# Tokenizer and attention of a vision tower: instruction order written by hand in place of the framework's scheduler

## The chip, the cores and the metric

The kernel runs on one core of one Trainium2 chip. A core has a matrix engine (TensorE, "PE" in the profile; its weight loads are listed apart as "PEld"), a vector engine (VectorE, "DVE"), a scalar engine (ScalarE, "ACT"), a general engine (GpSimd, "POOL") and a queue engine for transfers (SyncE, "SP"). Each engine runs its own stream of instructions in order and waits on semaphores for the others. On-chip memory is SBUF; PE writes into PSUM, eight banks of 128 partitions by 512 floats. The metric is the device time of one launch in microseconds (us), the median of several runs. Smaller is better.

## What is computed

32 images of 256 x 256 pixels become 256 tokens of 256 features each, and two transformer layers follow, all in float32. The change touches only the tokenizer, the attention of layer 0, and the first moments of layer 0's feed-forward part. Cut to these, the reference is:

```
# tokenizer: 16 x 16 patches of 3 channels -> 768 numbers per token
h = einsum('bnk,ek->bne', patches, W) + b

# layer 0, gated attention on layernorm(h); H = 512, S = 128
norm  = norm(x) * rsqrt(d);  xn = x / max(norm, 1e-5) * g
uv    = silu(xn @ W_uv + b_uv)                 # 256 -> 512 + 512 + 128
u, v, base = uv[:512], uv[512:1024], uv[1024:]
q, k  = base * gamma[0] + beta[0], base * gamma[1] + beta[1]
attn  = square(relu(q @ k.T * rsqrt(S)))
h     = h + (u * (attn @ v)) @ W_o + b_o

# layer 0, feed-forward with a router, on x = layernorm(h)
weights = x @ wr + br
sel     = the 127 tokens of each image with the largest weights
h       = h + x + (mlp(x[sel]) * weights[sel] at sel, 0 elsewhere)
# layer 1: a phase memory (part D) and a mixture of attention heads (part E)
...
```

## The kernel before

The parts follow one another: A is the tokenizer, B is layer 0's attention, C its feed-forward part, D and E are layer 1. The activations `H[b]` of all 32 images stay in SBUF for the whole run. The kernel is written in a framework that finds the waits by itself. It can also choose the order of the instructions within each engine's stream, from its own estimate of times. Where the code opens a `manual_schedule` for an engine, that engine's instructions keep the order in which they are written.

In the kernel before, part A is in written order for PE, ACT and SP only (DVE and POOL are ordered by the framework). Part B is ordered wholly by the framework. Parts C, D and E are in written order on all engines.

Part A handles one image at a time: 12 products (6 blocks of the 768 inputs, 2 halves of the tokens), an eviction with bias, and the statistics of the norm. Part B works on pairs of images. `unit_b` is a generator; each `yield` ends one step of a pair, and the steps of successive pairs are handed out so that up to five pairs are under way. The transposes and the products all go through `bank()`, a ring of the 8 PSUM banks.

```
def transposed(xT, xs, copy):              # 8 transposes into 2 banks, 2 copies
    for k in range(2):
        p = bank()
        for j, x in enumerate(xs):
            for c in range(NC):
                nc.tensor.transpose(p[:, ...], x[:, c, k * P : (k + 1) * P], ident)
        copy(k, xT[:, k, :], p[:, 0:w])    # copy_split: k = 0 on ACT, k = 1 on DVE

def unit_b(b0):                            # images b0 and b0 + 1
    xs = []
    for j in range(2):
        x = p4.tile([P, NC, D], F32, name="bx")
        normed(x, b0 + j, st_b)            # 2 tensor_scalar on DVE
        xs.append(x)
        nc.gpsimd.tensor_tensor(H[b0 + j], H[b0 + j], <b_o>, ALU.add)
    transposed(xT, xs, copy_split)
    <base: 2 products 128 x 512, silu on ACT>     # needs both halves of xT
    <q and k: 2 tensor_scalar on DVE>
    yield
    <scores: 4 products 128 x 256, relu on ACT, square on POOL>
    <gates uT: 8 products 128 x 512, silu on ACT>
    <values vs: 8 products 128 x 512, bias on DVE, silu on ACT>
    yield
    <gated: 16 products 128 x 256, times uT on DVE -> gT>
    if b0 == B - 2:
        turn_c(0, quads[0], 0)             # part C: transposes of the first four images
    <output: 16 products 128 x 256, added to H on DVE; statistics; power on POOL>
    yield
    normed_c[b0] = [norm_c(b0 + j) for j in range(2)]
    yield
    ranks(b0)                              # bank pw; rank_c for both images
    if b0 in (2, 6): first_ranks(b0 - 2, quads[b0 // 4], 0)

def norm_c(b):                             # layernorm for the router, and its weights w
    x = px.tile([P, NC, D], F32, name="cx", bufs=6)
    normed(x, b, st_c)
    nc.gpsimd.tensor_tensor(H[b], H[b], x, ALU.add)
    <per half: scalar_tensor_tensor with the row wr, summed into w, through a scratch ctmp>
    return x, w

def rank_c(b, x, w, pw):
    for c in range(NC):                    # w across the columns: 2 transposes on PE
        nc.tensor.transpose(pw[:, c * P : (c + 1) * P], w[:, c : c + 1].to_broadcast([P, P]), ident)
    <per half: 2 scalar_tensor_tensor on DVE that read pw, into ctmp, and a rank>
    <3 small DVE instructions; 2 indirect DMAs on POOL that store x by rank>
```

At the start of part C, in written order:

```
for t in range(END_C):
    if t < 2:
        ranks(B - 4 + 2 * t)               # pairs 28 and 30, which part B left
    if t == 0:
        normed_c[B - 2] = [norm_c(B - 2 + j) for j in range(2)]
    step_c(t)                              # t = 0: hidden_c(.., 0), t = 1: hidden_c(.., 1), ...
```

`hidden_c` is 8 products of 128 x 512 for each half, with a GELU on ACT. In the profile, line L115 is the helper of all products, L188 the transposes of `transposed`, L193 and L195 its copies on ACT and DVE, L174 the norms, L350 the transposes of `w`, L355 and L357 the ranks on DVE.

Of the kernel before, what the change touches and what calls it, by code (L numbers as in the profile page):

```python
# [33 lines left out]
F32 = mybir.dt.float32  # L34
# [6 lines left out]
P = 128  # L41
# [38 lines left out]
def vit_tower(tc, a, out):  # L80
# [115 lines left out]

    def one_step(active):
        return [g for g in active if next(g, g) is not g]

    def phase(unit, images, steps):  # L200

        active = []
        for b in range(0, B, images):
            active = one_step([unit(b)] + active)
        for _ in range(steps - 1):
            active = one_step(active)
        return active  # L210


    region, passing_x = ExitStack(), ExitStack()
# [33 lines left out]

    patches = a["patches"].rearrange("(k p) t -> p k t", p=P)
    with (
        tc.tile_pool(name="a_w", bufs=1) as pw,  # L250
        tc.tile_pool(name="a_x", bufs=6) as pp,
        tc.manual_schedule(engines={ENG.PE, ENG.Activation, ENG.SP}),
    ):
# [33 lines left out]

        loaded = []
        st_b = new_stats("b")

        def unit_a(b):
            if b == 0:
                ps = [bank() for _ in range(NC)]
                for k in range(n_k):
                    for c in range(NC):
                        mm(ps[c][:, 0:D], x0[k][:, c * P : (c + 1) * P], tokW[k], k == 0, k == n_k - 1)
                for c in range(NC):
                    nc.vector.tensor_tensor(H[b][:, c, :], ps[c][:, 0:D], row_a("tok_b"), ALU.add)
            else:
                x, p = xs_a.pop(b), bank()  # L300
                for c in range(NC):
                    for k in range(n_k):
                        mm(p[:, c * D : (c + 1) * D], x[:, k, c * P : (c + 1) * P], tokW[k], k == 0, k == n_k - 1)
                nc.vector.tensor_tensor(
                    H[b], p.rearrange("p (c d) -> p c d", c=NC), over(row_a("tok_b"), [P, NC, D], 1), ALU.add
                )
                if b + 5 < B:
                    load_patches(b + 5)
            st, _, i = at(st_b, b)
            for c in range(NC):  # L310
                stats(st, i, c, H[b][:, c, :])
            if b == 4:
                loaded.extend(layer_0_weights())
            if b % 2:
                factors_b(b - 1)
            yield

        def factors_b(b):


            st, rs, i = at(st_b, b)
            q = slice(i * NC, (i + 2) * NC)
# [4 lines left out]
            nc.gpsimd.tensor_tensor(rs[:, q], rs[:, q], minus_half[:, 0 : 2 * NC], ALU.pow)  # L327
            nc.vector.scalar_tensor_tensor(rs[:, q], low, 1e5, rs[:, q], ALU.mult, ALU.min)
            nc.vector.tensor_scalar(rs[:, q], rs[:, q], col("attn_g"), None, ALU.mult)

        phase(unit_a, 1, 2)
        wuv, row_b, wo, row_c, before, w1 = loaded

    def norm_c(b):
        x = px.tile([P, NC, D], F32, name="cx", bufs=6)
        normed(x, b, st_c)
        nc.gpsimd.tensor_tensor(H[b], H[b], x, ALU.add)

# [7 lines left out]
        return x, w  # L346

    def rank_c(b, x, w, pw):
        for c in range(NC):
            nc.tensor.transpose(pw[:, c * P : (c + 1) * P], w[:, c : c + 1].to_broadcast([P, P]), ident)  # L350

# [18 lines left out]
    with (  # L370
# [3 lines left out]
        st_c = new_stats("c")  # L374
        scale = 1.0 / math.sqrt(128.0)

        def unit_b(b0):
            xs = []
            for j in range(2):
                x = p4.tile([P, NC, D], F32, name="bx")  # L380
                normed(x, b0 + j, st_b)
                xs.append(x)
                nc.gpsimd.tensor_tensor(
                    H[b0 + j], H[b0 + j], over(row_b("b_o"), [P, NC, D], 1), ALU.add
                )
            xT = p2.tile([P, 2, 2 * N], F32, name="bxT")
            transposed(xT, xs, copy_split)

            base = p2.tile([P, 2 * N], F32, name="base")
            p = bank()  # L390
            for k in range(2):
                mm(p, wuv[:, k, 1024:1152], xT[:, k, :], k == 0, k == 1)
            nc.scalar.activation(base, p, AF.Silu, bias=col("b_base"))
            q = p2.tile([P, 2 * N], F32, name="bq")
            nc.vector.tensor_scalar(q, base, col("gamma", 0), col("beta", 0), ALU.mult, ALU.add)
            kk = p2.tile([P, 2 * N], F32, name="bk")
            nc.vector.tensor_scalar(kk, base, col("gamma", 1), col("beta", 1), ALU.mult, ALU.add)

            yield
            attn = []  # L400
            for j in range(2):
                p = bank()
                for m in range(NC):
                    mm(p[:, m * N : (m + 1) * N], kk[:, j * N + m * P : j * N + (m + 1) * P], q[:, j * N : (j + 1) * N])
                r = p2.tile([P, NC, N], F32, name="relu")
                nc.scalar.activation(r.rearrange("p m n -> p (m n)"), p, AF.Relu, scale=scale)
                t = p4.tile([P, NC, N], F32, name="attn")
                nc.gpsimd.tensor_tensor(t, r, r, ALU.mult)
                attn.append(t)

            uT = p2.tile([P, 4, 2 * N], F32, name="uT")
            for hc in range(4):
                p = bank()
                for k in range(2):
                    mm(p, wuv[:, k, hc * P : (hc + 1) * P], xT[:, k, :], k == 0, k == 1)
                nc.scalar.activation(uT[:, hc, :], p, AF.Silu, bias=col("b_u", hc))
            vs = []
            for tb in range(2 * NC):
                p = bank()
                for k in range(2):  # L420
                    mm(p, xT[:, k, tb * P : (tb + 1) * P], wuv[:, k, 512:1024], k == 0, k == 1)
                v = p4.tile([P, 512], F32, name="bv", bufs=8)
                nc.vector.tensor_tensor(v, p, row_b("b_v"), ALU.add)
                nc.scalar.activation(v, v, AF.Silu)
                vs.append(v)

            yield
            gTs = []
            for j in range(2):
                gT = p2.tile([P, 4, N], F32, name="gT")  # L430
                for half in range(2):
                    p = bank()
                    for h in range(2):
                        hc = 2 * half + h
                        for m in range(NC):
                            mm(
                                p[:, h * N : (h + 1) * N], vs[j * NC + m][:, hc * P : (hc + 1) * P],
                                attn[j][:, m, :], m == 0, m == NC - 1,
                            )
                    nc.vector.tensor_tensor(  # L440
                        gT[:, 2 * half : 2 * half + 2, :], p.rearrange("p (h n) -> p h n", h=2),
                        uT[:, 2 * half : 2 * half + 2, j * N : (j + 1) * N], ALU.mult,
                    )
                gTs.append(gT)
            if b0 == B - 2:
                turn_c(0, quads[0], 0)
            for j in range(2):
                b, gT = b0 + j, gTs[j]
                p = bank()
# [5 lines left out]
                for c in range(NC):  # L455
                    stats(st, i, c, H[b][:, c, :])

            pow_rstd_of(st_c, b0, 2)

            yield  # L460
            normed_c[b0] = [norm_c(b0 + j) for j in range(2)]

            yield
            ranks(b0)
            if b0 in (2, 6):
                first_ranks(b0 - 2, quads[b0 // 4], 0)

        normed_c = {}

        def ranks(b0):  # L470
            pw = bank()
            for j in range(2):
                rank_c(b0 + j, *normed_c[b0][j], pw[:, j * N : (j + 1) * N])


        phase(unit_b, 2, 3)
    region_b.close()

# [248 lines left out]
    with region_c:  # L727
# [20 lines left out]
        def fetch(b0, s, half):  # L748
            s.y = s.y if half else []
            for b in range(b0 + 2 * half, b0 + 2 * half + 2):  # L750
                y = px.tile([P, NC, D], F32, name="cx", bufs=6)
                for c in range(NC):
# [31 lines left out]
        preparing = prepare()  # L784
        with tc.manual_schedule(engines={ENG.PE, ENG.DVE, ENG.Activation, ENG.Pool, ENG.SP}):
            for t in range(END_C):
                if t < 2:
                    ranks(B - 4 + 2 * t)
                if t == 0:
                    normed_c[B - 2] = [norm_c(B - 2 + j) for j in range(2)]  # L790
                if t == END_C - 2:
                    norm_d(0, pairs[0], px, "cx", 6)
                step_c(t)
                if t >= 8:
                    next(preparing, None)
        passing.close()
# [5 lines left out]
    with (  # L802
        tc.manual_schedule(engines={ENG.PE, ENG.DVE, ENG.Activation, ENG.Pool, ENG.SP}),
        tc.tile_pool(name="d_2", bufs=2, reuse_waits="tile") as p2,
# [119 lines left out]
    right_d.close()  # L924
    passing_x.close()


# [719 lines left out]
```

## Time and profile before

| | before |
|---|---|
| time, median of 3 runs | 2030.3 us (2027.38 to 2031.56) |
| span of the profiled run | 2025.9 us |
| PE busy | 1953.6 us (96%) |
| DVE / ACT / POOL busy | 1316.5 / 823.9 / 726.8 us |
| PE records | 15108 products and as many weight loads |

A float32 product appears as two records in the trace (the tokenizer's 384 products as 768). [...] the records of a dense stream overlap, so the time that a stream takes is read from its length and not from the sum of durations. In the stage table each row gives, for one stretch, its length, then for PE, PEld, DVE, ACT and POOL the busy us with the number of instructions that started there, then the granted clock of PE (1.00 is full speed), the share of DMA and the GB/s. In the timeline each row gives the start, the length of a merged run of like instructions, engine, line, operation, output<-input and count; in square brackets stand the idle us ahead of it and what ended them.

### The profile page before, as it was taken

What the parts mean: (1) busy time and instruction counts of PE and PEld (TensorE: products, weight loads), DVE (VectorE), ACT (ScalarE), POOL (GpSimd) and SP (SyncE); (2) the same over time, 40 slices, a digit from 0 to 9 for tenths busy, and PEclk for the clock granted to TensorE, in tenths of its full rate; (3) what the DMA queues carried; (4) which work ended last, traced back from release to release, by engine and by line L of the source; (5) the groups of instructions that cost most, each with busy time, mean ns of one, the idle gap of its engine ahead of it and who ended that gap; (6) DMA issues with size and microseconds to landing.
All of it is one profiled execution on the core that took longest, in us unless ns stands there. A gap on an engine that the chain in (4) does not pass through costs nothing.

```text
span 2025.9 us, 37649 instructions
## 1 busy us (share of the span) xinstructions
PE 1953.6 (96%) x15108; PEld 1374.2 (68%) x15108; DVE 1316.5 (65%) x3605; ACT 823.9 (41%) x1549; POOL 726.8 (36%) x692
## 2 busy tenths in 40 slices
PE   9998999999999989999899999999999999999984
PEld 8885676766666757666455555577777777777762
DVE  2335557676665653443556465567889999998986
ACT  0001312122222112212444444377777777777761
POOL 1224215243432342434333433203444443434443
PEclk9999999999999999999899999999999999999996
DMA  9440000000000141221000000001212121221211
GB/s 301 150 139 1 0 0 32 16 27 11 22 13 19 36 147 50 78 68 58 11 0 1 1 1 0 0 23 33 54 49 59 49 59 49 54 54 46 62 49 54
DMA packets 69813, 95.09 MB, mean 47 GB/s; under 512 B 8576, under 2 KB 51200, under 8 KB 69248
## 3 DMA queue, kind: packets, MB, share of 16 engines
q1 hardware_dynamic: 62912, 75.04, 13.0%
q0 software_dynamic: 6144, 16.79, 2.7%
q8 instruction: 121, 1.98, 0.4%
q10 hardware_dynamic: 576, 0.79, 0.1%
q14 instruction: 60, 0.49, 0.1%
HBM read 46.45 MB, written 20.97 MB: 33 GB/s over the span
## 4 chain that ended last, share of the span: by engine, by line
PE 94%; DVE 3%; ACT 1%; DMA 1%; POOL 0%; issue 0%; SPq 0%; ACTq 0%; DVEq 0%
PE bank L115 88%; PE bank L688 2%; PE bank L188 1%; PE bank L1192 1%; PE bank L350 0%; DMA both<-hx 0%; ACT bxT L193 0%; PE bank L241 0%; DVE fout L1201 0%; DMA tokW<-in_tokW_dram 0%; DVE bx L174 0%; DVE ctmp L357 0%; DVE fout L1197 0%; DVE two L1123 0%; DVE ctmp L355 0%
## 5 line engine op out<-in xcount | busy, mean ns | idle before, releaser
L1040 ACT ACTIVATE et<-bank 128x512 f32<-128x512 f32 x384 | 202.3, 598 | 58.5 <-DVE bank L1038 57.9
L115 PEld LDWEIGHTS bank<-ev,et 128*64 128x64 f32 x6144 | 198.4, 137 | 33.3 <-ACT et L1040 20.6
L115 PE MATMUL bank<-ev,et 128*64 128x74 f32 (+1 forms) x6144 | 211.3, 227 | 0.0
L1038 DVE TENSOR_TENSOR bank<-bank,w_tri 128x256 f32<-128x256 f32 (+1 forms) x384 | 173.6, 515 | 55.6 <-PE bank L115 53.7
L1118 POOL TENSOR_TENSOR eo<-eo,gate 128x1024 f32<-128x1024 f32 x64 | 121.9, 1925 | 215.7 <-DVE gate L1115 203.1
L115 PE MATMUL bank<-g,sx 64*128 64x512 f32 (+1 forms) x512 | 191.0, 502 | 1.4 <-ACT g L998 1.4
L115 PE MATMUL bank<-g,sw 64*128 64x512 f32 (+1 forms) x512 | 189.6, 502 | 0.0
L115 PE MATMUL bank<-tokW,patch 128*128 128x256 f32 x768 | 168.0, 382 | 0.3 <-DMA tokW<-in_tokW_dram 0.3
L115 PEld LDWEIGHTS bank<-tokW,patch 128*128 128x128 f32 x768 | 146.8, 191 | 21.6 <-DMA tokW<-in_tokW_dram 1.3
L115 PE MATMUL bank<-bxT,w_wuv 128*128 128x512 f32 x320 | 147.9, 601 | 6.6 <-ACT bxT L193 4.0
L193 ACT COPY bxT<-bank 128x512 f32<-128x512 f32 x16 | 9.4, 586 | 341.4 <-PE bank L188 341.4
L1070 POOL TENSOR_TENSOR hv<-hv,minus_half 128x8 f32<-128x8 f32 x64 | 119.6, 1868 | 5.3
L1056 ACT COPY eo<-bank 128x286 f32<-128x286 f32 x256 | 97.3, 421 | 58.5 <-PE bank L115 52.0
L115 PE MATMUL bank<-wvo,dm 128*128 128x512 f32 x256 | 114.0, 598 | 0.0
L115 PE MATMUL bank<-xsel,w_w 128*128 128x512 f32 x256 | 113.4, 601 | 0.0
L115 PE MATMUL bank<-attn,bv 128*128 128x256 f32 x512 | 113.3, 379 | 0.0
L115 PE MATMUL bank<-w_wo,gT 128*128 128x256 f32 x512 | 113.1, 379 | 0.0
L115 PE MATMUL bank<-w_w,hT 128*128 128x256 f32 x512 | 113.1, 379 | 0.0
L115 PE MATMUL bank<-w_wuv,bxT 128*128 128x512 f32 x256 | 112.5, 592 | 0.0
L115 PEld LDWEIGHTS bank<-attn,bv 128*128 128x128 f32 x512 | 97.1, 190 | 19.5 <-issue 6.7
L115 PEld LDWEIGHTS bank<-w_w,hT 128*128 128x128 f32 x512 | 96.7, 190 | 15.8 <-issue 3.4
L1069 POOL TENSOR_SCALAR hv<-ranges 128x8 f32<-128x8 f32 x64 | 39.1, 610 | 189.8 <-DVE ranges L1131 189.6
(258 smaller groups left out, 3861.8 us busy)
## 6 DMA issues: line engine op xcount, KB each, us to landing
patch<-in_patches_dram SPq DMA_DIRECT2D x31, 768.0 KB, 4.8
sw<-sx SPq DMA_DIRECT2D x64, 128.0 KB, 2.4
both<-fxT SPq DMA_DIRECT2D x64, 128.0 KB, 2.4
both<-hx SPq DMA_DIRECT2D x64, 128.0 KB, 2.3
out_dram<-fout SPq DMA_DIRECT2D x32, 256.0 KB, 2.4
cs<-ranked SPq DMA_DIRECT2D x32, 128.0 KB, 3.8
results<-cy SPq DMA_DIRECT2D x32, 128.0 KB, 1.7
w_w<-in_w_dram SPq DMA_DIRECT2D x2, 1024.0 KB, 6.1
```

The source lines that it names most:

```text
L115: nc.tensor.matmul(o, lhsT, rhs, start=first, stop=last)
L188: nc.tensor.transpose(p[:, o : o + P], x[:, c, k * P : (k + 1) * P], ident)
L193: nc.scalar.copy(o, i)
L688: nc.tensor.transpose(p[:, o : o + P], x[:, c, k * P : (k + 1) * P], ident)
L1038: nc.vector.tensor_tensor(own, own, over(tri, [P, n_e, P], 1), ALU.add)
L1040: nc.scalar.activation(t, p, AF.Exp)
L1056: nc.scalar.copy(im.o[:, c * NH + n, 0:OC], p[:, 0:OC])
L1069: nc.gpsimd.tensor_scalar(v, x, 1.0 / HD, 1e-8, ALU.mult, ALU.add)
L1070: nc.gpsimd.tensor_tensor(v, v, minus_half, ALU.pow)
L1118: nc.gpsimd.tensor_tensor(im.mix[k], im.mix[k], over(im.gate[:, :, 2 * k : 2 * k + 2], [P, NC * NH, 2, HD], 3), ALU.mult)
L1192: nc.tensor.transpose(im.po[:, o : o + P], im.fT[:, k, c * P : (c + 1) * P], ident)
```

## The change

All of the kernel from the tokenizer on is put in written order for PE, DVE, ACT, POOL and SP. For that, part B's generator becomes separate functions, one for each piece of a pair's work, and a loop over steps calls them in a chosen order. Four things are meant by that order:

- The norm of a pair (`norm_b`) is written in the middle of the step before the one that transposes it. Pair 0's and pair 1's norms are done inside the tokenizer, and pair 0's transposes, base, queries and keys are written ahead of the tokenizer's last image.
- The router weights of both images of a pair are transposed in one go (`turn_weights`) ahead of the scores, and the ranks that read them come after.
- The scores of the older pair are written between the transposes and the base product of the newer pair.
- The router's norms (`norms_c`) are written ahead of the values' evictions; for pair 28 they come ahead of the last output.

No instruction's arithmetic changes. The tiles of the norm in B move from a pool of four (`bx`) to the shared pool `cx`, which grows from 6 to 8. Pair 0's tiles borrow space of part C (`xsel`, `cs`).

```
+    by_hand.enter_context(tc.manual_schedule(engines={ENG.PE, ENG.DVE, ENG.Activation, ENG.Pool, ENG.SP}))
...
+        for b in range(B):                          # the tokenizer's loop
+            if b == B - 1:
+                half = [p0.tile(..., name="cs", bufs=2) ... for _ in range(2)]
+                turn_b(0, pairs_b[0], p0, "xsel")
+                base_b(0, pairs_b[0], half[0][:, 0 : 2 * N])
+                queries_b(0, pairs_b[0], half[0][:, 2 * N :], half[1][:, 0 : 2 * N])
+            unit_a(b)
+            if b == 4:
+                wuv, row_b, wo, row_c, before, w1 = layer_0_weights()
+            if b % 2:
+                powers = powers_b(b - 1)
+            elif b:
+                factors_b(*powers)
+            if b in (B - 6, B - 4):
+                u = (b - B + 6) // 2
+                norm_b(2 * u, pairs_b[u])
+                bias_b(2 * u, pairs_b[u])
...
-        x = px.tile([P, NC, D], F32, name="cx", bufs=6)
+        x = px.tile([P, NC, D], F32, name="cx", bufs=8)
...
-        phase(unit_b, 2, 3)
+        for t in range(B // 2 + 2):
+            new, old, older, next_one = pair(t) if t else None, pair(t - 1), pair(t - 2), pair(t + 1)
+            next_one = next_one if t else None
+            if new:
+                turn_b(*new, p2, "bxT")
+            if t >= 4:
+                turned = turn_weights(2 * (t - 4))
+            if old:
+                scores_b(*old)
+            if new:
+                base_b(*new, p2.tile([P, 2 * N], F32, name="base"))
+            if t >= 4:
+                ranks(2 * (t - 4), turned)
+                if t in (5, 7):
+                    first_ranks(2 * t - 10, quads[t // 2 - 2], 0)
+            if new:
+                queries_b(...)
+            if old:
+                gates_b(*old)
+            if t == 1:
+                factors_b(*powers)
+            if next_one:
+                norm_b(*next_one)
+            if old and t >= 3:
+                norms_c(2 * (t - 3))
+            if old:
+                values_b(*old)
+            if next_one:
+                bias_b(*next_one)
+            if old and t >= 3:
+                residuals_c(2 * (t - 3))
+            if older:
+                gated_b(*older)
+                if t == B // 2 + 1:
+                    turn_c(0, quads[0], 0)
+                    norms_c(2 * (t - 3))
+                    residuals_c(2 * (t - 3))
+                output_b(*older)
...
+        for t in range(END_C):                      # the start of part C
+            if t < 2:
+                ranks(B - 4 + 2 * t, turn_weights(B - 4 + 2 * t))
+            if t == 0:
+                norms_c(B - 2)
+                residuals_c(B - 2)
```

## The prediction

> **What bounds the kernel now.** I read the engine shares and the chain of waits first, then PE's timeline for the stretches where PE has idle time, then a table of stages cut at those stretches.
>
> ```profile
> PE 1953.6 (96%) x15108; PEld 1374.2 (68%) x15108; DVE 1316.5 (65%) x3605; ACT 823.9 (41%) x1549; POOL 726.8 (36%) x692
> PE 94%; DVE 3%; ACT 1%; DMA 1%; POOL 0%; issue 0%; SPq 0%; ACTq 0%; DVEq 0%
> ```
>
> PE is the bound nearly everywhere: 94% of the chain that ended last is PE's own work. The change removes no product, so all that it can win is time in which PE stands idle or runs below its full rate in parts A to C. The stage table says where that is:
>
> ```profile
> 172.20:189.80 17.60, 10.20 (x32) 5.57 (x33) 15.36 (x28) 4.23 (x6) 11.95 (x11) 0.90 0.00 0
> 189.80:203.50 13.70, 13.70 (x33) 6.03 (x32) 3.87 (x5) 5.32 (x9) 3.68 (x3) 1.00 0.01 1
> 203.50:681.80 478.30, 473.14 (x1713) 310.43 (x1712) 305.95 (x758) 114.38 (x178) 168.21 (x158) 1.00 0.05 16
> 681.80:711.20 29.40, 29.29 (x143) 25.46 (x142) 19.20 (x57) 2.50 (x3) 8.56 (x10) 1.00 0.23 60
> 711.20:731.60 20.40, 10.88 (x29) 5.04 (x28) 15.69 (x64) 2.75 (x4) 8.05 (x9) 0.83 0.61 211
> 745.40:2025.90 1280.50, 1231.86 (x12343) 863.98 (x12341) 895.01 (x2497) 690.69 (x1345) 481.79 (x427) 0.98 0.15 40
> ```
>
> Compare the first two figures of a row, length and PE busy. There are two holes: the tokenizer's end (172.2 to 189.8 us, 7.4 us idle, clock 0.90) and the start of part C (711.2 to 731.6, 9.5 us idle, clock 0.83). Part B between them is idle for only 5.2 of 478.3 us. The 48.6 us idle after 745.4 belong to code that is not touched.
>
> The first hole in PE's timeline:
>
> ```profile
> 173.37 0.41 PE L188 MATMUL bank<-ident,bx 128*128 128x128 f32 x2 [1.20 <-DVE bx L174]
> ...
> 180.81 1.71 PE L115 MATMUL bank<-bxT,w_wuv 128*128 128x512 f32 x2 [2.69 <-DVE bxT L195]
> ...
> 187.04 0.67 PE L115 MATMUL bank<-bq,bk 128*128 128x256 f32 x2 [1.60 <-DVE bk L397]
> ```
>
> After the last tokenizer product PE waits for the norm `bx`, then for the copy `bxT`, then for the keys `bk`, all on DVE: the first pair's chain norm, transpose, base, queries lies open. And the second:
>
> ```profile
> 714.59 0.43 PE L350 MATMUL bank<-ident,cw 128*128 128x128 f32 x2 [2.90 <-DVE ctmp L357]
> 719.48 0.69 PE L350 MATMUL bank<-ident,cw 128*128 128x128 f32 x2 [4.46 <-DVE ctmp L357]
> 719.96 9.01 PE L115 MATMUL bank<-xsel,w_w 128*128 128x512 f32 x16
> ...
> 731.34 0.43 PE L350 MATMUL bank<-ident,cw 128*128 128x128 f32 x2 [2.15 <-DVE ctmp L357]
> ```
>
> PE transposes one image's weights, waits until DVE has ranked that image (L357, which reads the same bank), transposes the next, and only then goes on to the feed-forward products. Those first 16 take 9.01 us; the next 16 took 7.03.
>
> In the steady state of part B, the chain and PE's timeline show a period of 33.06 us and small stalls:
>
> ```profile
> 537.31 27.98 PE bank L115 x98
> 570.36 27.98 PE bank L115 x98
> ```
> ```profile
> 566.62 1.13 PE L115 MATMUL bank<-bxT,w_wuv 128*128 128x512 f32 x2 [0.24 <-ACT bxT L193]
> 569.93 0.19 PEld L350 LDWEIGHTS bank<-ident,cw 128*128 128x128 f32 x2 [0.86 <-DVE ctmp L357]
> ```
>
> The base product follows its transposes at once and waits for the copy; the second image's weight transposes wait for the first image's ranks.
>
> [...] behind 2.90 and 4.46 us of waiting the stage's clock is 0.83. So a closed hole pays more than its idle time. [...] So the order written for DVE decides, and one late instruction holds all behind it; this is the risk here. [...] at 185.0 us `bq` took 0.53 us, while `bk`, of the same shape, took 1.48 beside a POOL addition and 1.75 in the mean. I use the longer durations.
>
> **The change part by part.** The rate of a dense stream comes from merged runs: 16 records of 512 columns took 7.03 us, the last lasting 0.59, so (7.03 - 0.59) / 15 = 0.429 us each; 32 of 256 columns took 7.07, so (7.07 - 0.38) / 31 = 0.216; 8 transposes took 1.04, so (1.04 - 0.27) / 7 = 0.11.
>
> *Tokenizer to part B.* From 172.2 to 203.5, in 31.3 us, PE does two pairs' transposes and bases and one pair's scores, gates and values. In the new order, pair 0's transposes (8 x 0.11 = 0.9) and base (4 records, 1.7) stand ahead of the last image. That base still follows its transposes at once, and its second copy queues on DVE behind the image's eviction (0.69), statistics (1.05) and factors (0.4): 0.7 us of copy on top makes about 2.8, against 1.75 for PE; I add 0.8 us of waiting. After the image come pair 1's transposes (0.9), pair 0's scores (8 records, 1.7), pair 1's base (1.7), then gates and values (32 records, 13.7). The queries had the whole of an image (5.2 us between evictions) to be made. Sum 2.6 + 0.8 + 4.3 + 13.7 = 21.4; the gain is **9.9 us**.
>
> *Steady part B.* Per step PE has 36 records of 512 columns (15.4), 72 of 256 (15.6) and 12 transposes (1.3): 32.3 us dense against 33.06, so 0.76 is the most to be won. The scores (1.7 us) now fill the time of the copies, and weights turned in one go need no ranks in between. Some seams stay, where the kind of product changes; I take 0.5 of the 0.76, for 12 steps with weights: 6.0. The first three steps have 31.9 dense against 32.37 measured: 0.3 each. The one longer step, 636.5 to 670.8, holds a wait of 1.41 us of the same cause, but its end overlaps the next step; I leave it out and round to **7 us**.
>
> Does DVE keep up in written order? From the step's start: the tail of the last output (addition, statistics) to 2.0 us; copy of xT to 2.7, while base's second half needs it at 0.9 + 0.4 + 1.7 + 0.9 = 3.9, so there is 1.2 us to spare; ranks of two images 4.8 to 7.5; queries and keys 2.5 to 10; norm of the next pair 4 x 0.6 to 12.4; router norms 4 x 0.59 + 4 x 0.7 + 0.8 = 6 to about 18. The values' first eviction, whose bank is ready at about 14, thus runs 4 us late. This costs nothing: the last of four is done at about 20, and the ring of eight banks asks for the first one again only with the output, after 25 us; the values are used a step later. DVE is then level with PE in `gT`.
>
> *Part B to C.* Pair 28's router norms now come ahead of the last output on DVE, so its weights are ready when that output ends (call it E, 711.2 before). PE can transpose them (0.5) and go straight to 16 feed-forward records (6.9): busy to E + 7.4. Pair 30's weights take longer: last addition and statistics to E + 2.0, ranks of pair 28 (2.37 an image, 4.75) to E + 6.8, norms of pair 30 (3.6 in this stretch, up to 4.4) to E + 10.4 or 11.2. So PE waits 3 to 4 us at the second step of C, because the transposes are written ahead of that step's products. The second half of the products starts at about E + 11.6, before at E + 20.4. Minus up to 1 us for a clock that falls again: **8 us**.
>
> Sum: 9.9 + 7 + 8 = 24.9 us; 2030.3 - 24.9 = 2005.4, and I put 2006. The later parts are bound by PE and their order is unchanged, so the gain is carried to the end.
>
> **The rivals.** (1) *Written order stalls PE in every step.* The scheduler could place one DVE instruction of a rank between two others; a fixed order can't. If the copy of xT were 1 us too late for base in each of 15 steps, 15 us would go: about 2021. For it: [...] 1.2 us to spare is little. Against: the stalls before come to 5.2 us in all, and DVE has some 7 us of idle time a step. (2) *The wait at the start of C moves rather than shrinks*: loads for the later parts and ranks collide, or the clock falls; then only 4 us of 8: 2010. The SP stream issues about 30 loads there, of some 0.5 us each, and the first store of results stands behind them; before they ended at E + 11, and the store is needed only at about E + 20. (3) *More comes than I count*: all of the 0.76 per step, and no wait at C: 2030 - 34 = 1996. (4) *The gain is lost later*, where transfers meet other work: the chain is PE's, so I give this little.
>
> **Range and chances.** Rival 1 at half its size with rival 2 gives about 2017, rival 3 gives 1996; I take 1997 to 2018. Faster by over 2% means below 1989.7, or 40.6 us, more than PE's idle time up to 745 us (7.4 + 5.2 + 9.5, and 1.5 in the first 20 us) with some 4 us of slow clock. Slower by over 2% would need new stalls of 65 us.
>
> **What would show it.** Right: PE's timeline has no wait over 1 us between the last tokenizer product and the second step of part B; the period of part B is 32.4 to 32.7 us; base has no wait for `bxT` and the weight transposes none for `ctmp`; at the start of C a single wait of 3 to 4 us stands ahead of the second pair of weight transposes. Wrong: PE waits for the DVE copy of xT or for a bank in every step, or a period at or over 33.06; a wait ahead of the first feed-forward products; or a later part that grows.

## The result, and the profile after

The changed kernel takes 2001.63 us (median of 4 runs, 2001.15 to 2002.32), the kernel before 2029.88 (now the median of 4 runs): a ratio of 0.9862, 95% interval 0.9845 to 0.9879. That is about 28 us, 1.4%, so within 2%. The predicted time was 2006, the range 1997 to 2018. The profiled runs differ by 25.6 us (2025.9 and 2000.3); the readings below account for this figure.

The page's lines of engine shares and of the chain:

```profile
PE 1942.6 (97%) x15108; PEld 1373.5 (69%) x15108; DVE 1289.7 (64%) x3605; ACT 824.6 (41%) x1549; POOL 722.7 (36%) x692
PE 94%; DVE 4%; DMA 1%; ACT 0%; issue 0%; SPq 0%; POOL 0%; ACTq 0%; DVEq 0%
```

The counts of PE, DVE, ACT and POOL are those of before; only times moved. Note DVE: the same 3605 instructions are busy for 26.8 us less. The stage table, cut at the places that answer to those of before (length, then PE busy; the last three figures are the clock, the DMA share and GB/s):

```profile
167.80:181.40 13.60, 12.70 (x58) 9.27 (x57) 6.08 (x16) 4.34 (x6) 1.89 (x4) 1.00 0.00 0
195.10:662.40 467.30, 467.30 (x1717) 312.13 (x1716) 282.42 (x780) 114.81 (x178) 170.70 (x164) 1.00 0.05 17
691.40:703.40 12.00, 8.33 (x26) 3.70 (x25) 11.05 (x45) 2.75 (x4) 3.21 (x6) 1.00 0.83 256
703.40:718.90 15.50, 15.50 (x51) 9.70 (x50) 7.17 (x19) 2.75 (x4) 9.26 (x10) 0.89 0.33 105
```

In the second row length and PE busy are equal: over some 14 steps of part B, PE has no idle time at all. The hole at the tokenizer's end keeps 0.9 us of 7.4, the hole at part C's start 3.7 of 9.5, and the stage behind the latter runs at a clock of 0.89. Taking the same piece of work in both timelines gives the account:

| up to | before | after | won in this stretch |
|---|---|---|---|
| third pair's transposes (start of step 2) | 203.54 | 195.14 | 8.4 |
| `gated` of the last full step | 681.82 | 662.40 | 11.0 |
| weight transposes behind the last output | 711.09 | 691.35 | 0.3 |
| second half of part C's first products | 731.61 | 703.37 | 8.5 |
| the products behind them | 738.48 | 711.93 | -1.7 |
| end | 2025.9 | 2000.3 | -0.9 |

PE's timeline where the holes were: first the tokenizer's end, then the start of part C.

```profile
169.16 1.12 PE L115 MATMUL bank<-xsel,w_wuv 128*128 128x512 f32 x2 [0.24 <-ACT xsel L193]
170.95 1.12 PE L115 MATMUL bank<-xsel,w_wuv 128*128 128x512 f32 x2 [0.66 <-DVE xsel L195]
...
692.03 7.03 PE L115 MATMUL bank<-xsel,w_w 128*128 128x512 f32 x16
701.60 0.40 PE L482 MATMUL bank<-ident,cw 128*128 128x128 f32 x2 [2.54 <-DVE cw L378]
703.10 0.43 PE L482 MATMUL bank<-ident,cw 128*128 128x128 f32 x2 [1.09 <-DVE cw L378]
703.37 8.73 PE L115 MATMUL bank<-xsel,w_w 128*128 128x512 f32 x16
```

The first two lines are pair 0's base, waiting for the two copies of its transposes. The third shows the feed-forward products running at once and at full rate; then PE waits for pair 30's router weights, and the next 16 records need 8.73 us instead of 7.03. In the steady state the chain has one unbroken run of 108 records a step, at a period of 32.30 us:

```profile
551.07 30.99 PE bank L115 x108
583.37 30.99 PE bank L115 x108
```

### The profile page after: what moved, and what is told of

It reads as the page before. It is cut to its first block, busy times and chain, and to the rows that moved or that the text cites. A ratio compares the mean times of both kernels' runs of the same rounds, so it can differ in the third digit from the quotient of the medians.

```text
span 2000.3 us, 37646 instructions
## 1 busy us (share of the span) xinstructions
PE 1942.6 (97%) x15108; PEld 1373.5 (69%) x15108; DVE 1289.7 (64%) x3605; ACT 824.6 (41%) x1549; POOL 722.7 (36%) x692
## 4 chain that ended last, share of the span: by engine, by line
PE 94%; DVE 4%; DMA 1%; ACT 0%; issue 0%; SPq 0%; POOL 0%; ACTq 0%; DVEq 0%
PE bank L115 89%; PE bank L750 2%; PE bank L188 1%; PE bank L1254 1%; DMA both<-hx 0%; DMA patch<-in_patches_dram 0%; PE bank L229 0%; PE bank L482 0%; DVE fout L1263 0%; DVE ctmp L375 0%; DVE two L1185 0%; DVE fout L1259 0%; DVE ctmp L391 0%; DVE ctmp L389 0%; DVE six L123 0%
## 5 line engine op out<-in xcount | busy, mean ns | idle before, releaser
L115 PEld LDWEIGHTS bank<-ev,et 128*64 128x64 f32 x6144 | 198.2, 137 | 33.2 <-ACT et L1102 20.6
L115 PE MATMUL bank<-bxT,w_wuv 128*128 128x512 f32 x300 | 131.4, 592 | 0.0
L123 DVE BATCH_NORM_STATS2 six<-h 128x6 f32<-128x256 f32 x256 | 105.5, 412 | 4.4
L115 PEld LDWEIGHTS bank<-w_wo,gT 128*128 128x128 f32 x512 | 97.2, 190 | 13.2
```

The costliest lines, as they stand in the source:

```text
L115: nc.tensor.matmul(o, lhsT, rhs, start=first, stop=last)
L123: nc.vector.bn_stats(six, x)
```

## The experiments

Each run is a whole kernel that computes the full result. Ratios are to the kernel before, with 95% intervals; "the changed kernel" is at 2001.63 us, ratio 0.9862 (0.9845 to 0.9879). The kernel before, run again beside them, took 2027.96 to 2029.57 us, so a difference of 2 us between two of these runs means nothing.

### Base directly behind the transposes

```
 turn_b(*new, ...)
+base_b(*new, ...)
 turn_weights(...); scores_b(*old)
-base_b(*new, ...)
```

> The changed kernel with one thing undone: in each step of part B the base product stands right behind the transposes again, and the weight transposes and the older pair's scores come after it. Theory (the scores hide the copies of xT): VectorE's copy ends about 2.5 us after a step begins, base's second half could start at about 1.3; so PE waits 0.24 for ScalarE's copy and 1.0 to 1.2 for VectorE's in each of 14 steps, period 33.5 to 34.0 us instead of 32.30, time 2001.6 + 14 x 1.4 = about 2021. Rival (any written order will do[...]): period within 0.3 of 32.30, time under 2006.

2017.79 us, 0.9943 (0.9927 to 0.9960): 16 us given back. PE's timeline in one step:

```profile
597.38 1.12 PE L115 MATMUL bank<-bxT,w_wuv 128*128 128x512 f32 x2 [0.24 <-ACT bxT L193]
598.84 1.12 PE L115 MATMUL bank<-bxT,w_wuv 128*128 128x512 f32 x2 [0.33 <-DVE bxT L195]
```

The step's transposes start at 596.11, the next step's at 629.51: the period is 33.40, 1.10 more than with the scores in between. The waits are only 0.57 of this. The rest is what a wait does to a stream: records that follow each other closely overlap, and at a break they don't. Two records take 1.12 us when they stand alone and 2 x 0.429 = 0.86 in a dense stream. Counted from start to start, the transposes at 596.11 take 1.27 us instead of 0.87, the first two records 1.46 and the second two 0.96 (the weight transposes follow at 599.80) instead of 0.86 each: 1.10 in all. The theory holds; the wait for VectorE was a third of the expected one, the breaks made up for part of it, and the period stayed just under the expected 33.5.

### Router weights one image at a time, in one bank and in two

```
-turned = turn_weights(2 * (t - 4))      # ahead of the scores
...
-ranks(2 * (t - 4), turned)
+for j in range(2):                      # behind base
+    p = <first image's bank>            # second run: p = bank() for each image
+    <2 transposes of w into p>; rank_c(b0 + j, x, w, p[...])
```

> The changed kernel with the router weights transposed one image at a time again, into one shared bank, each image's ranks directly behind its transposes, at the place of the ranks (behind base). Theory (the second image's transposes wait until VectorE has read the first image's out of the same bank): the first rank starts about 4.5 us after a step begins and takes 2.1, PE stands about 2.2 us in each of 14 steps and once at the place where the pair's weights are the last in part B: period about 34.4, time about 2030. Rival (the number of separate turns does not matter): period within 0.3 of 32.30.

> As the run that transposes one image's weights at a time, but each image's transposes go into a bank of their own. Theory (the shared bank is the cause): nothing waits for the ranks, period 32.3 to 32.6, time within 4 us of 2001.6. Rival (it is the in-order place behind base that costs, or the split as such): as slow as the one with the shared bank, about 2030.

One bank: 2045.38 us, 1.0082 (1.0065 to 1.0099). Two banks: 2000.53 us, 0.9857 (0.9840 to 0.9873), not to be told from the changed kernel. PE's timeline with one bank:

```profile
618.40 0.43 PE L497 MATMUL bank<-ident,cw 128*128 128x128 f32 x2 [2.15 <-DVE ctmp L391]
618.67 7.03 PE L115 MATMUL bank<-bxT,w_wuv 128*128 128x512 f32 x16
...
653.34 8.73 PE L115 MATMUL bank<-bxT,w_wuv 128*128 128x512 f32 x16
```

The second image's transposes wait 2.15 us, as computed, until VectorE has read the first image's out of that bank; the step's period is 34.67, and 36.37 where the products behind the same wait run slowly, as in the last line. With two banks the four transposes run as one piece of 0.60 us. So it is the shared bank that made PE wait, not the number of turns nor their place. The slowdown of 44 us against the changed kernel, for which 28 was expected, is more than the 31.7 us of these waits. Behind five of the thirteen waits of 2.15 us, and behind the last one of 3.71, the products run 1.7 us longer; in these six stretches the granted clock is 0.80 or 0.81, behind the other eight waits it is 1.00. Six times 1.7 is 10.2 us. A break of 0.2 us (34.67 - 32.30 - 2.15) at each of the 14 waits brings the sum to about 45.

### Norm of the next pair at the start of its own step

```
+if t > 1: norm_b(*new); bias_b(*new)
 turn_b(*new, ...)
...
-norm_b(*next_one)                       # mid-step
```

> The changed kernel with the norm of a pair (and its bias addition) written at the start of the step that transposes it instead of in the middle of the step before. Theory (VectorE's order decides): VectorE is busy with the last output's addition and statistics until 1.9 us into a step and the norms take 1.4 to 2.4, so the transposes start 3.3 to 4.3 us late in each of 14 steps: period about 36, time 2045 to 2065, more if the granted clock falls behind these waits. Rival (VectorE has 7 us of slack a step and PE hides it): under 2006.

2062.88 us, 1.0164 (1.0141 to 1.0188): slower than the kernel before.

```profile
599.22 1.74 PE L188 MATMUL bank<-ident,cx 128*128 128x128 f32 x8 [2.30 <-DVE cx L174]
601.50 3.30 PE L115 MATMUL bank<-bq,bk 128*128 128x256 f32 x8
...
636.37 1.74 PE L188 MATMUL bank<-ident,cx 128*128 128x128 f32 x8 [2.30 <-DVE cx L174]
638.38 1.89 PE L115 MATMUL bank<-bq,bk 128*128 128x256 f32 x8
```

The wait is 2.30 us, less than expected, but the step from 599.22 to 636.37 lasts 37.15, so 4.85 us are lost in it. The work behind the wait runs slowly: the scores take 3.30 us, at a clock of 0.57, against 1.89 in a dense stretch. The next step has the same wait, but its scores keep 1.89 us, and it lasts 35.47. The 2.30 us are the wait for the first norm only: the first transposes follow the norms one by one, with three more waits of 0.18 from 636.37 on, so the eight take 1.74 us instead of 1.04. Of eleven periods eight are near 37.1 and three near 35.5; the mean is 36.67, a loss of 4.4 us a step. The place of the norm in the middle of the step before is worth more than the whole gain of the change.

### Pair 28's router norms behind the last output

```
-norms_c(28); residuals_c(28)
 output_b(*older)
+norms_c(28); residuals_c(28)
```

> The changed kernel with pair 28's router norms written behind the last output of part B instead of ahead of it. Theory: the weights of pair 28 are ready about 5 us after that output's end, PE waits these 5 us ahead of part C's first products and then hardly at the second place (3.6 us now), the first products may run at a reduced clock: 2 to 4 us slower than 2001.6. Rival (the placing is what brings most of the 8.4 us won there): 8 us slower.

2004.92 us, 0.9878 (0.9862 to 0.9895): about 3 us slower, as expected, though the interval overlaps that of the changed kernel. PE now waits 3.65 and 3.20 us ahead of part C's first products, of which 16 records take 9.18 us, and no longer at the second place. The placing brings a part of the gain only: from the end of the last output to the products behind the second half it is 27.4 us before, 24.2 here and 20.6 in the changed kernel. That the rest comes from turning both images' weights in one go is not shown by this run; the old text with a second bank (below) needs 22.8 us there, which points the same way.

### Where the gain at the tokenizer's end comes from

Two runs: pair 0's transposes, base and queries behind the last image; and in addition the norms of pairs 0 and 1.

```
 for b in range(B):
-    if b == B - 1: turn_b(0, ...); base_b(0, ...); queries_b(0, ...)
     unit_a(b)
-    if b in (B - 6, B - 4): norm_b(...); bias_b(...)      # second run only
+<norm_b(0), bias_b(0)>                                     # second run only
+turn_b(0, ...); base_b(0, ...); queries_b(0, ...)
+<norm_b(2), bias_b(2)>                                     # second run only
```

> The changed kernel with pair 0's transposes, base and queries written behind the tokenizer's last image instead of ahead of it; the norms of pairs 0 and 1 stay inside the tokenizer. Theory A (most of the 8.4 us won at this border comes from norms made early): base waits 1.4 us for the copy, the scores 2 us for the queries, 0.9 us of waiting ahead of the last image goes: 2 to 4 us slower than 2001.6. Theory B (it comes from pair 0's whole chain standing ahead of the last image): 7 to 9 us slower.

> The changed kernel with pair 0's whole chain behind the tokenizer's last image, norms included, and pair 1's norms behind its queries. Theory (the early norms are what the border's gain comes from, as the run with only transposes, base and queries moved cost 1.5 us at most): PE waits 3 us for the norms, then for copy and queries, and pair 1's transposes wait for its norms: 7 to 10 us slower than 2001.6. Rival: within 3 us of it, the gain at the border would then come from the scheduler's former mixing of other work into VectorE's stream.

The first takes 2003.17 us, 0.9876 (0.9860 to 0.9893), no clear difference; step 2 of part B starts at 195.03 us, in the changed kernel at 195.14. PE waits 0.24, 0.32 and 1.04 us behind the last image instead of 0.24 and 0.66 ahead of it. In this run the tokenizer's own products end about 1 us earlier than in the changed kernel, so for equal starts the place ahead of the last image is worth about 1 us, too little to show in the times. The second takes 2012.16 us, 0.9915 (0.9899 to 0.9932), 10.5 us over the changed kernel where 7 to 10 were expected, and step 2 starts at 203.90:

```profile
175.58 1.65 PE L188 MATMUL bank<-ident,cx 128*128 128x128 f32 x8 [2.38 <-POOL low L148]
```

So the gain here goes when the early norms go (203.90 - 195.14 = 8.8, with the tokenizer's products ending at the same time in both): about 8 us are those of the norms, about 1 that of pair 0's place.

### Old and new text, scheduler and written order

Two runs complete a square with the two kernels: the new text with the framework's scheduler in part B's loop, and the old text in written order in parts A and B.

```
# new text, scheduler in part B
+by_hand.close()                         # ahead of part B's loop
...
+by_hand.enter_context(<manual_schedule>) # behind it

# old text, written order
-tc.manual_schedule(engines={ENG.PE, ENG.Activation, ENG.SP})     # part A
+tc.manual_schedule(engines=<all five>)                           # parts A and B
```

> The changed kernel's text as it is, but the framework orders all engines in part B's loop again; tokenizer and part C stay in written order. Theory (the hand-written order inside a step is what removed the stalls): period back to about 33 us, time 2001.6 + 8 to 14 us. Rival (the restructured text, with norms and turns earlier in the program, is enough for the scheduler too): period 32.3 to 32.5, time within 3 us of 2001.6.

> The kernel before, its text unchanged, but with tokenizer and part B in written order on all engines. With the run that gives the changed text to the scheduler this completes a square of old or new text, scheduler or written order. Theory (the moves in the text are what counts; written order as such is worth nothing): in the old text a pair's norm, transposes, base and queries stand in one row at the start of a step, so PE waits for VectorE's norms (2.3 us measured when they are late), the copies (0.6) and, where one image's weights are turned after the other's ranks, 2.2 more: 5 us or more of waiting in each of 16 steps and a slower clock, time 2090 or more. Rival (written order itself brings the gain): faster than 2029.

| | scheduler in part B | written order |
|---|---|---|
| old text | 2029.88 | 2240.23, 1.1041 (1.1022 to 1.1060) |
| new text | 2004.92, 0.9878 (0.9861 to 0.9894) | 2001.63 |

With the new text the scheduler reaches the same steady state as the written order. Its chain, and its PE timeline at the tokenizer's end:

```profile
560.13 30.99 PE bank L115 x108
592.43 30.99 PE bank L115 x108
```
```profile
176.97 2.07 PE L115 MATMUL bank<-xsel,w_wuv 128*128 128x512 f32 x2 [4.93 <-DVE xsel L195]
```

The period is 592.43 - 560.13 = 32.30. What it loses is one wait of 4.93 us and about 3 us of slow work behind it (the last image's 24 records take 7.47 us here and 5.34 in the changed kernel): in DVE's timeline nine norms (L174) run between 165.8 and 176.2 us, ahead of the copy that PE waits for. At part C's start it is the better one, with waits of 0.36 and 1.09 and no slow products behind them. The old text in written order waits in every step, with a period of 47.8:

```profile
573.35 0.69 PE L350 MATMUL bank<-ident,cw 128*128 128x128 f32 x2 [9.02 <-DVE ctmp L357]
576.85 2.30 PE L188 MATMUL bank<-ident,bx 128*128 128x128 f32 x8 [2.81 <-DVE bx L174]
```

So my theory for the first of the two runs falls and its rival holds for the period; the time, 3.3 us over the changed kernel's, just misses its 3. The new text brings nearly all of the gain; written order adds about 3 us to it, if anything, and with the old text it costs 210 us. Two things go with the new text in this square and are not parted from the moves: the pool `cx` of 8 tiles, and the tokenizer in written order on DVE and POOL too.

### The kernel before with a second bank

```
-pw = bank()
 for j in range(2):
-    rank_c(b0 + j, *normed_c[b0][j], pw[:, j * N : (j + 1) * N])
+    rank_c(b0 + j, *normed_c[b0][j], bank()[:, 0:N])
```

> The kernel before, with the scheduler, and only a bank of its own for each image's weight transposes. Theory (the shared bank causes the 0.86 us wait of each step and most of the hole at part C's start): the steps lose part of their 0.76 us, the waits of 2.90, 4.46 and 2.15 at part C's start shrink, 8 to 14 us faster than the kernel before. Rival (the scheduler's order keeps VectorE late anyway, or the waits move to the norms of the router): within 4 us of it.

2020.75 us, 0.9957 (0.9941 to 0.9974): this one change to the old text is worth 8.4 us. Runs of 108 records follow at 567.77 and 600.58 in its chain, a period of 32.81. Of the 0.76 us that a step could win, the bank had cost 0.25; the other 0.51 are the base product's wait for its copy and the breaks around it. At part C's start waits of 4.76 and 0.75 us remain, but the stretch there is 4.6 us shorter (22.8 against 27.4), more than half of the gain.

### The last waits in parts A to C

One run moves only the residual additions of pair 28; the other also takes away the rest by order.

```
# residual later
-norms_c(28); residuals_c(28); output_b(*older)
+norms_c(28); output_b(*older)
 <part C, t = 0:> ranks(28, ...); norms_c(30)
+residuals_c(28)
 residuals_c(30)

# in addition
+pair 0: turn_b ahead of image 30, base_b and queries_b ahead of image 31
+pair 30: ranks(30, turn_weights(30)) behind step_c(1) instead of ahead of it
```

> The changed kernel with one thing moved: the two residual additions of pair 28 on GpSimd come behind the norms of pair 30, so they no longer run beside the router norms of pair 28, one of whose instructions took 3.05 us instead of 0.42 there. Theory (GpSimd's addition held VectorE[...] and so made PE wait): weights of pair 30 are ready 2.6 us earlier, PE's waits at part C's start fall from 3.6 to about 1.1 us and the clock stays up: 3 to 4 us faster than 2001.6. Rival (the long instruction waited for something else): no change.

> The changed kernel with its remaining waits in parts A to C taken away by order alone: pair 0's transposes one image ahead of its base; pair 30's weights transposed behind the second half of the feed-forward products; the residual additions of pair 28, which hold VectorE up for 2.6 us[...], behind the norms of pair 30. Theory: the waits of 0.9 and 3.6 us go and the granted clock stays at 1.00 (1.7 us): 4 to 6 us faster than 2001.6. Rival (the wait moves on to the stores of ranked rows or the results): within 2 us of 2001.6.

In the changed kernel DVE's timeline and POOL's show this during the last output:

```profile
688.38 3.05 DVE L375 SCALAR_TENSOR_TENSOR ctmp<-cx,rows_c 128x256 f32<-128x256 f32 x1
```
```profile
688.65 2.49 POOL L382 TENSOR_TENSOR h<-h,cx 128x512 f32<-128x512 f32 x2
```

The same DVE instruction takes 0.42 us just before. With the two POOL additions moved away all four take 0.41 or 0.42, pair 30's weights come earlier, PE's waits fall from 2.54 and 1.09 to 0.96 and 1.09, and the products behind them take 7.03 us. The time is 1998.42, 0.9848 (0.9831 to 0.9864): 3.2 us less. An addition that no one waits for, on an engine with a third of its time used, had cost PE 3 us through VectorE: 1.58 of waiting and 1.70 of slow products. The overlap and its removal are shown; how the two engines hold each other up is not. By the records the instruction began 0.27 us ahead of the additions and ended just behind them (691.43 against 691.14 us).

The run with all moves takes **1994.65 us**, 0.9832 (0.9816 to 0.9849), against before 33 us. It beats both kernels: 6 to 7 us below the changed kernel (6 by the ratios, 7 by the times), where 4 to 6 were expected. From 15 us on to 780 us PE has no wait, and part C starts with its two halves in one piece:

```profile
690.26 13.90 PE L115 MATMUL bank<-xsel,w_w 128*128 128x512 f32 x32
```

## Why the prediction was right, and where it was not

**The bound.** Right: PE's own work is 94% of the chain before and after, no record of it went away, and the gain is idle time and slow clock in parts A to C. The later part gave 0.9 us back, close to nothing, as the fourth rival's small weight said. That the sum came out so near is in part luck: 24.9 us were predicted and 25.6 are in the profiles, but the three terms missed by -1.5, +4.0 and -1.2 us.

**Tokenizer to part B, predicted 9.9.** Measured 8.4. The waits behind pair 0's transposes are 0.24 and 0.66, counted as 0.8 (the prediction's own figures, 2.8 against 1.75, give 1.05). About 1 us went at the very start of the run, where a wait of 2.76 us for a first load stands in the changed kernel's profile and one of 0.31 in that of before. It is not the change's: the old text with a second bank has one of 2.04. The other half us is in the breaks of the stream. But the reason given was too wide: the early norms bring about 8 us, pair 0's place ahead of the last image about 1.

**Steady part B, predicted 7.** Measured 11.0; this term was mis-sized. I took 0.5 of the 0.76 us a step on the ground that seams between kinds of product stay. They don't: transposes, weight transposes and products follow each other at the dense rate, and the period is exactly the dense 32.3, below the 32.4 to 32.7 named as a sign of being right. I also left out the long step of 1.4 us, which came back in full.

**DVE's budget.** The conclusion, no stall, was right, its figures too high. VectorE does start its instructions in the order of the text: in the step from 551 us the copy at 551.61, the ranks from 552.18, the queries from 557.49, the norms from 558.41, the router norms from 559.70, the values' evictions from 563.14. I took the long durations of before for queries (2.5), norms (2.4) and router norms (6); in the new order they take 1.0, 1.3 and 3.3. Fewer of them run long: of the 224 normalizing, scaling and weighting instructions of these groups 77 took over 1.4 times the shortest of their kind before, and 11 do now; all 88 overlap a POOL addition or squaring of 128x512 (43 of the short ones before overlapped one too). An example: `bk` took 2.00 us at 539.47 before, while POOL squared `attn` (540.12, 1.05 us), and takes 0.53 at 557.95 now, with no arithmetic on POOL beside it. The records of these three groups sum to about 56 us less than before in the whole kernel; DVE as a whole is only 26.8 us less busy; the casts of the ranks (L361, now L395) grew from 6.3 to 16.5 us. The values' first eviction is not 4 us late but waits for PE. The spare time for the copy of xT, put at 1.2 us, is about 1.4: the copy ends at 584.57, base's second half is due at about 585.95.

**Part B to C, predicted 8.** 8.5 less the 1.7 of slow clock (0.63 from 703.4 to 708 us), so 6.8. The one wait of 3 to 4 us came where it was foreseen, 3.6 in two pieces, but for a mixed reason: the norms are quicker than I had them, and an instruction held up by POOL for 2.6 us, which I had not seen coming, filled the difference.

**The rivals.** The first, a stall in every step, did not come, and the runs with base first and with late norms show it was a real one: 16 and 61 us for one misplaced call. Its argument, that a scheduler can do what a fixed order can't, was beside the point: given the new text the scheduler reaches the same period. The second came in part, by the clock. The third came for the steady state.

## What to carry to other kernels

Where one engine is the bound, look in its timeline for the short waits beside dense runs, and move what it waits for a step earlier in the program; whether the framework or the text then orders the stream mattered little here (3 us), but written order without these moves was 10% slower. Two results that one bank holds and another engine reads tie the second producer to the first reader (a wait of 2.15 us a step here, none with two banks): give each its own bank, or write both before the first is read. And a call on an engine that nobody waits for is not always free (two additions on POOL cost 3.2 us here): place it where the engine that it can hold up has nothing urgent.

## What was not expected of the hardware

A wait cost more than its length here. Two waits of 0.57 us together cost 1.10, since the records on the two sides of a break no longer overlap (1.12 us for two that stand alone, 0.86 in the dense stream). Norms that PE had to wait for, 2.30 us and three times 0.18, cost 3.2 us where the scores behind them kept their 1.89 us, and up to 4.85 where they took 3.30, at a clock of 0.57.

In the run with the shared bank the same wait of 2.15 us stands in a dense stream thirteen times: behind five the next 16 records took 8.73 us, at a clock of 0.80 or 0.81, behind eight 7.03, at 1.00. So the length of a single wait did not settle whether the clock fell. What does, these runs leave open.
